# An RWKV block and a gated FFN on one core: the first block of tokens normed and mixed in two halves, sums named apart from mixes, and background work that passes what is blocked

## The chip, the core and the metric

The kernel runs on one core of a Trainium2 chip. The metric is the device time of one execution in microseconds (us). The engines are TensorE (PE in the profile; its weight loads are PEld), VectorE (DVE), ScalarE (ACT), GpSimd (POOL) and SyncE (SP). Each takes its own instructions in order. SP, ACT and POOL issue the DMAs of this kernel.

## The reference

The input has 2048 tokens of 512 channels in float32. An outer layer norm without weights stands ahead of each of two layers, and each layer is added to its input.

```
x = x + L0_attn(layernorm(x));  x = x + ffn(layernorm(x))

L0_attn(x): h = layer_norm(x, g1, b1);  hh = h shifted by one token
  k = (h*mk + hh*(1-mk)) @ Wk.T;  v, r the same with mv, mr
  x = x + sigmoid(r) * wkv(k, v) @ Wo.T
  h = layer_norm(x, g2, b2);  hh = h shifted by one token
  kk = (h*ck + hh*(1-ck)) @ Wkey.T;  kv = silu(kk) @ Wval.T
  x = x + sigmoid((h*cr + hh*(1-cr)) @ Wcr.T) * kv
ffn(h): gate, up = h @ w_gate_up.T;  (silu(gate) * up) @ w_down.T
```

So each layer begins with two norms in a row. For a token with variance v they come to (x - mean) times one inverse root of v(1+eps)+eps^2, and the residual needs the inverse root of v+eps.

## The kernel before, in words

The tokens are worked in NB = 4 blocks of 512 (NT = 4 tiles of 128 tokens). All weights are 512x512 squares, 25 of them, each kept as four quarters. A product of a block with a square is a unit. Units of the first two blocks for Wk, Wr, Wv, Wo are plain (`plain_unit`, L555): four quads (i, j) of output, where j is the half of the tokens and i the half of the output channels, and four chunks kc of 128 input channels each. One pass over a (kc, quad) pair is two calls of the matmul in L573, and the trace shows each call as two records of 128x256. A plain unit has 64 records. All other units (`unit`, L453) use seven products of half-size blocks in place of eight (56 records). For that they need sums of the activation's blocks, T1 to T4 (`sums_of`, L377: four DVE subtractions in L303), and sums of the weights, which `prepare` (L111) makes in the background and keeps in HBM. In a unit, `snapshot` (L488, ACT) copies a bank of PSUM before the next product adds to it, so PE waits for it.

The order on PE, DVE and ACT is that of the Python program (`manual_schedule`). Work that no unit needs at once is written as generators. `push` (L245) appends one to the list `background`; `urgent` (L248) puts it in front. Each unit calls `tick` (L227) after each product, or after each second chunk of a plain quad (8 ticks a plain unit). A tick adds SHARE*STEP = 0.88*1.72 = 1.51 us to an account, `slack`, capped at 2.5, takes off what was issued since, by the kernel's own cost table (0.68 for a 128x512 DVE operation), and while it is positive runs steps of `preps` or of the head of `background` (`run_one`, L165). A `yield 1` ends the tick, so that a result has time to arrive. `need` (L251) runs the head of the list, whatever the account says, until a name is in `finished`.

An entry may have a condition, `ready`. `run_one` asks it before every step of the entry, not only before the first:

```
        ready, gen, name = background[0]
        if ready is not None and not ready():
            assert not wait, name
            return False
```

For a mix it is `op_free` (L385): fewer than three of three large operand tiles are in use. A mix takes its tile in its first step (`op_tile`, L388); `op_done` gives it back when the unit that reads it issues its last product, which for a `unit` is some products later, inside the next unit (`held`, `pop_held`).

`mix` (L397) makes h*m + hh*(1-m), by chunk of channels: an ACT copy with scale (`shifted`, L406, 128x512) and a DVE multiply-add (`mixed`, in `stt`, L311). `mix_steps` (L427) then also makes the four sums, unless the unit is plain, and the name counts as finished only after them. So `need((b, name))` in `product_of` (L593) waits for the sums too.

The beginning is written out by hand. L260 loads the vectors (20 KB) on ACT's queue; L261 loads the first block of x on SP's and ACT's queues by turns; L262 to L264 load Wk, Wr, Wv. L273 issues 44 transposes of the identity (`WARM`), which nothing reads. Then `time_norm` (L624) runs for block 0 by `need("norm0")`: moments of four tiles (L317, L318), the inverse roots of 128x8 by shift, subtraction and three Newton steps on DVE (`rsqrt`, L323), four scalings (L307), 16 transposes on PE (L354), for each chunk an ACT evacuation from PSUM (L366) and, for block 0, the k mix of that chunk at once. `k_unit(0)` follows with its chunks as the outer loop. From then on norms, mixes and residuals (`residual`, L607) are background work, also those of block 1 (`norm1`).

Later, during the four up units of block b, these entries stand in the list in this order: norm b+2, mix k of b+2, residual of b+2, mix r, norm b of b+1 (`normb`), mix v of b+2, mixes cr and ck of b+1. The down unit of b follows, then the k, r and v units of b+2, then the gate unit of b+1.

Of the kernel before, what the change touches and what calls it, by code (L numbers as in the profile page):

```python
# [15 lines left out]
P = 128  # L16
H = 512
NC = H // P
# [37 lines left out]
def rwkv_ffn_kernel(  # L56
# [107 lines left out]

    def run_one(wait):  # L165

        ready, gen, name = background[0]
        if ready is not None and not ready():
            assert not wait, name
            return False  # L170
        try:
            r = next(gen)
        except StopIteration:
            background.popleft()
            finished.add(name)
            return True
        return wait or r is None
# [67 lines left out]
    def push(name, gen, ready=None):  # L245
        background.append((ready, gen, name))

    def urgent(name, gen):  # L248
        background.appendleft((None, gen, name))
# [8 lines left out]

    vec = const.tile([P, NVEC, NC], F32, name="vec")
    nc.scalar.dma_start(vec, vecs)  # L260
    xin = {0: load_x(0, (nc.sync, nc.scalar, nc.sync, nc.scalar))}  # L261
# [52 lines left out]
    def moments(src, mv):  # L314
        for t in range(NT):
            st = small.tile([P, 6], F32, tag="st", name="st")
            nc.vector.bn_stats(st, src[:, t, :])  # L317
            nc.vector.bn_aggr(mv[:, t, :], st)  # L318
            cost(512)
            cost(0)  # L320
            yield
# [39 lines left out]
    def shifted_norm(s, h, hT, g, b, then=None):  # L361
# [3 lines left out]
        def evacuate(c, pt):  # L365
            nc.scalar.activation(  # L366
                hT[:, c, 1:], pt, AF.Identity, bias=vcol(b, c), scale=vcol(g, c)
            )
            if then is not None:
                then(c)  # L370
# [17 lines left out]
    def op_tile(name):  # L388
# [3 lines left out]
        return m, [m[:, k] for k in range(7)]  # L392
# [4 lines left out]
    def mix(key, hT, row, plain=False, at_once=False):  # L397
        m, B = op_tile("mix")
        ops[key] = B

# [22 lines left out]
        if at_once:  # L423
            return lambda c: (shifted(c), mixed(c))
        return mix_steps(B, shifted, mixed, plain)

    def mix_steps(B, shifted, mixed, plain):  # L427
# [3 lines left out]
        for c in range(NC):  # L431
# [3 lines left out]
            yield  # L435
        if not plain:
            yield from sums_of(B)
# [117 lines left out]
    def plain_unit(n, B, sink, by_token, done=None, free=None, chunks_first=False):  # L555
# [4 lines left out]
        if chunks_first:  # L560
            order = [(kc, [q]) for kc in range(NC) for q in quads]
        else:
            order = [(kc, [q]) for q in quads for kc in range(NC)]
        for kc, qs in order:
            kb, k = divmod(kc, 2)
            for i, j in qs:
# [25 lines left out]

    def product_of(b, n, name, sink, by_token, done=None, free=op_done):  # L593
        if (b, name) not in ops:
            flush()
        need((b, name))
        B = ops.pop((b, name))
        if b < PLAIN and n <= WO:
            plain_unit(n, B, sink, by_token, done, free, b == 0 and name == "k")
# [7 lines left out]
    def residual(b, xb, mv, rstd):  # L607
        shift = small.tile([P, NT], F32, tag="shift", name="shift")
        tt(shift, mv[:, :, 0], rstd, ALU.mult)
        ts(shift, shift, -1.0, None, ALU.mult)  # L610
        x1 = tok_tile("x1")
        x1s[b] = x1
        for t in range(NT):
            nc.scalar.activation(
                x1[:, t, :],
                xb[:, t, :],
                AF.Identity,
                bias=shift[:, t : t + 1],
                scale=rstd[:, t : t + 1],
            )  # L620
            spent[0] += 0.4
            yield

    def time_norm(b):  # L624
# [3 lines left out]


        var = small.tile([P, 2 * NT], F32, tag="var2", name="var2")  # L630
        ts(var[:, :NT], mv[:, :, 1], EPS, None, ALU.add)
        ts(var[:, NT:], mv[:, :, 1], 1.0 + EPS, EPS * EPS, ALU.mult, ALU.add)
# [7 lines left out]
        tails[b] = residual(b, xb, mv, rstd)  # L640
        if b == 0:
            constants()
            then = mix((0, "k"), hT, MK, True, True)
            finished.add((0, "k"))
            yield from shifted_norm("a", h, hT, LN1G, LN1B, then)
        else:
            yield 1
            yield from shifted_norm("a", h, hT, LN1G, LN1B)
# [3 lines left out]
    def push_residual(b):  # L652
# [3 lines left out]
        push(("x1", b), run())  # L656
# [5 lines left out]
    def push_mix(b, name, gen):  # L662
        push((b, name), gen, op_free)
# [34 lines left out]
    def hidden_sums(key, q, plain=False):  # L698
        B = {B11: q[0, 0], B12: q[0, 1], B21: q[1, 0], B22: q[1, 1]}
        ops[key] = B  # L700
        if plain:
            finished.add(key)
        else:
            for t in (T1, T2, T4):
                B[t] = q_tile("t")
            urgent(key, sums_of(B))
# [54 lines left out]
    def up_unit(b, g):  # L761
        s = {}

        def sink(i, j, c):
# [6 lines left out]
            [ops[b, "ck"]],  # L771
# [7 lines left out]

    class Lazy:  # L780


        def __init__(self, key):
            self.key = key

        def __getitem__(self, b):
            while self.key not in ops:
                assert put_off, self.key
                flush()
            if b in (T1, T2, T3, T4):  # L790
                while self.key not in finished:
                    run_one(True)
            return ops[self.key][b]
# [23 lines left out]
    def ffn_in(b):  # L817
# [23 lines left out]
        yield from transposed(z, evacuate)  # L841
        yield 1
# [4 lines left out]
    def ffn_gate(b, g):  # L847
# [7 lines left out]
        unit([WG + g], [ops[b, "z"]], sink, False)  # L855

    def ffn_up(b, g):
        s = gated.pop((b, g))

        def sink(i, j, c):  # L860
# [4 lines left out]
            [ops[b, "z"]],  # L865
# [38 lines left out]
    push("norm0", time_norm(0))  # L904
    need("norm0")
# [21 lines left out]
    for b in range(NB):  # L927
# [28 lines left out]
        if b == NB - 1:  # L956
            push(("ffn", 0), ffn_in(0), op_free)
# [4 lines left out]
    for b in range(NB):  # L962
        for g in range(4):
            if b == 0 or g > 0:
                need(("ffn", b))
# [4 lines left out]
            if g == 1 and b + 1 < NB:  # L970
                push(("ffn", b + 1), ffn_in(b + 1), op_free)
        if b + 1 < NB:
            need(("ffn", b + 1))
# [59 lines left out]
```

## Time and profile before

| | |
|---|---|
| median of 3 runs | 1285.92 us (1285.86 to 1288.44) |
| the profiled execution | 1284.93 us, of it span 1283.2 us |
| PE busy | 1260.0 us, 98% |
| DVE, ACT, POOL busy | 51%, 27%, 9% |
| mean granted TensorE clock | 0.997 |

The span runs from the first to the last instruction; some 1.7 us of the execution lie outside it. A line of the timeline gives the start and length in us, the engine, the line of the code, the operation, the tile written and those read, how many instructions are merged, and in brackets the idle time of the engine before it with what ended that. A line of the waits gives the total in us, how often, and the longest. A line of the windows gives busy time of each engine in a stretch of the span, then the granted clock, the busy share of the DMA engines and GB/s. Records of L573 follow each other every 0.217 us on PE when nothing is missing.

### The profile page before, as it was taken

The page shows a single profiled execution, that of the slowest core. Times are in us where ns is not written, and L with a number is a line of the kernel's source. Part 1 is how long each engine was busy: PE and PEld are TensorE (multiplying, and loading weights), DVE is VectorE, ACT ScalarE, POOL GpSimd, SP SyncE. Part 2 cuts the span into 40 slices and gives each one's busy share as a digit, 9 for nine tenths or more (in the row PEclk, how much of TensorE's full clock was granted, in tenths as well). Part 3 has the DMA queues.
Part 4 walks back from the last instruction along what each step waited for, and adds up shares of the span by engine and source line. Part 5 has one row for each costly group of instructions (what it writes and reads, how often), then busy time and mean ns, then how long its engine had stood idle before and what let it go on. Part 6 is the DMA issues. An engine that isn't in the chain of part 4 may idle for free.

```text
span 1283.2 us, 16131 instructions
## 1 busy us (share of the span) xinstructions
PE 1260.0 (98%) x5900; PEld 1104.4 (86%) x5900; DVE 650.4 (51%) x1173; ACT 344.4 (27%) x579; POOL 117.7 (9%) x218
## 2 busy tenths in 40 slices
PE   8999999989999899999999999999999999999998
PEld 7788888878888788888888888888888888888886
DVE  4757667467674586733563375125631374123521
ACT  5443251343423433302311232012310122102200
POOL 1222221200121111121100000000000000000000
PEclk9999999999999999999999999999999999999999
DMA  4656787765677677688755745575456554565552
GB/s 174 237 187 201 255 265 248 240 215 172 210 237 228 225 221 236 209 281 292 235 158 178 224 148 152 155 247 152 146 151 226 176 154 145 151 178 160 155 152 70
DMA packets 121374, 251.72 MB, mean 196 GB/s; under 512 B 15056, under 2 KB 16080, under 8 KB 120272
## 3 DMA queue, kind: packets, MB, share of 16 engines
q1 hardware_dynamic: 103328, 193.51, 50.1%
q0 software_dynamic: 16960, 55.59, 11.9%
q10 hardware_dynamic: 1008, 1.59, 0.3%
q8 instruction: 48, 0.79, 0.3%
q14 instruction: 30, 0.25, 0.1%
HBM read 216.03 MB, written 34.60 MB: 195 GB/s over the span
## 4 chain that ended last, share of the span: by engine, by line
PE 95%; DVE 3%; ACT 1%; issue 0%; DMA 0%; ACTq 0%
PE ps L471 84%; PE ps L573 9%; PE ps L354 2%; DVE mix L311 1%; DVE u L303 1%; DVE mix L303 1%; DMA x<-in_x 0%; ACT s L488 0%; ACT mix L406 0%; DVE h L307 0%; DVE st L317 0%; ACT r L675 0%; DVE resid L303 0%; DVE e L303 0%; ACT e L680 0%
## 5 line engine op out<-in xcount | busy, mean ns | idle before, releaser
L471 PE MATMUL ps<-zT,w 128*128 128x256 f32 x1792 | 391.0, 379 | 0.0
L471 PEld LDWEIGHTS ps<-zT,w 128*128 128x128 f32 x1792 | 340.0, 190 | 46.0
L471 PE MATMUL ps<-mix,w 128*128 128x256 f32 x1232 | 275.4, 381 | 7.4 <-ACT s L488 5.7
L471 PEld LDWEIGHTS ps<-mix,w 128*128 128x128 f32 x1232 | 233.7, 191 | 43.2 <-ACT s L488 7.3
L471 PE MATMUL ps<-w,s 128*128 128x256 f32 x1024 | 228.0, 379 | 0.7 <-ACT u L488 0.7
L471 PEld LDWEIGHTS ps<-w,s 128*128 128x128 f32 x1024 | 194.3, 190 | 27.4 <-ACT u L488 1.1
L303 DVE TENSOR_TENSOR u<-ps,u 128x512 f32<-128x512 f32 x135 | 93.3, 691 | 227.8 <-PE ps L471 225.4
L488 ACT COPY u<-ps 128x512 f32<-128x512 f32 x136 | 79.3, 583 | 455.1 <-PE ps L471 454.9
L471 PE MATMUL ps<-w,t 128*128 128x256 f32 x816 | 181.6, 379 | 3.3 <-ACT s L488 2.5
L471 PEld LDWEIGHTS ps<-w,t 128*128 128x128 f32 x816 | 154.6, 190 | 25.2 <-ACT s L488 3.3
L303 DVE TENSOR_TENSOR s<-ps,s 128x512 f32<-128x512 f32 x84 | 57.9, 689 | 157.1 <-PE ps L471 136.1
L303 DVE TENSOR_TENSOR u<-u,u 128x512 f32<-128x512 f32 x68 | 46.8, 688 | 84.2 <-ACT u L488 84.1
L573 PE MATMUL ps<-mix,w 128*128 128x256 f32 x384 | 85.4, 385 | 4.1 <-issue 3.0
L573 PEld LDWEIGHTS ps<-mix,w 128*128 128x128 f32 x384 | 73.9, 193 | 14.8 <-issue 3.2
L128 POOL DMA_DIRECT2D sum<-raw x64 | 34.9, 546 | 262.4 <-DVE raw L303 248.4
L488 ACT COPY s<-ps 128x512 f32<-128x512 f32 x68 | 39.2, 576 | 60.4 <-PE ps L471 60.4
L881 POOL DMA_DIRECT2D out<-resid x12 | 8.6, 715 | 497.6 <-DVE resid L303 487.6
L471 PE MATMUL ps<-w,mix 128*128 128x256 f32 x224 | 51.8, 380 | 0.0
L303 DVE TENSOR_TENSOR raw<-raw 128x512 f32<-128x512 f32 x64 | 43.9, 686 | 13.4 <-DMA raw<-in_w 12.9
L471 PEld LDWEIGHTS ps<-w,mix 128*128 128x128 f32 x224 | 42.1, 190 | 6.7 <-DVE mix L311 0.7
L117 POOL DMA_DIRECT2D raw<-in_w x64 | 34.3, 542 | 124.8 <-PE ps L471 118.5
L303 DVE TENSOR_TENSOR t<-s,t 128x512 f32<-128x512 f32 x64 | 44.3, 692 | 2.1
(100 smaller groups left out, 811.2 us busy)
## 6 DMA issues: line engine op xcount, KB each, us to landing
w<-sum SPq DMA_DIRECT2D x368, 256.0 KB, 2.7
w<-in_w SPq DMA_DIRECT2D x304, 256.0 KB, 2.8
raw<-in_w POOLq DMA_DIRECT2D x64, 256.0 KB, 5.1
sum<-raw POOLq DMA_DIRECT2D x64, 256.0 KB, 3.7
q<-in_w POOLq DMA_DIRECT2D x36, 256.0 KB, 5.2
sum<-q POOLq DMA_DIRECT2D x36, 256.0 KB, 3.1
x<-in_x SPq DMA_DIRECT2D x30, 256.0 KB, 5.1
res<-x SPq DMA_DIRECT2D x4, 1024.0 KB, 6.2
```

Source lines behind the costliest of these rows:

```text
L117: paced(nc.gpsimd.dma_start(t, w[n, k]))
L128: nc.gpsimd.dma_start(sums[n][k], o)
L303: nc.vector.tensor_tensor(out, a, b, op)
L311: nc.vector.scalar_tensor_tensor(out, *args)
L354: nc.tensor.transpose(flat[:, t * P : (t + 1) * P], h[:, t, c * P : (c + 1) * P], ident)
L471: mm = nc.tensor.matmul(pz[:, m, :], lhsT=lhsT, rhs=rhs, start=first and g == 0 and m == 0 and k == 0, stop=g == last and k == 1, skip_gro ...
L488: nc.scalar.copy(tmp[name], acc["z"])
L573: mm = nc.tensor.matmul(acc[i, j][:, m, :], lhsT=act[:, k, lo] if by_token else wg[:, k, lo], rhs=wg[:, k, :] if by_token else act[:, k, : ...
L881: eng.dma_start(out_t[b][:, 2 * j : 2 * j + 2, i * HB : (i + 1) * HB], rs[b][:, 2 * j : 2 * j + 2, i * HB : (i + 1) * HB],)
```

## The change

The load of the vectors is moved behind the load of the first block of x on ACT's queue. `run_one` looks at the first three entries of the list; an entry that has begun is not asked its condition again, an entry that is not ready lets later entries with no condition, or begun ones, run, and after a `yield 1` the next entry gets a step in the same call. A mix is finished by its own name when it is mixed, and its entry, with the sums, has the name (b, name, "t"). `Lazy` (moved up, now used for all operands) runs the background until that entry is finished when a unit first asks for one of T1 to T4. Mixes and the residual get "the norm is finished" as a condition. The residual computes its shift by tile. Block 0 gets a function of its own, in place of `time_norm(0)`, and the second half of it is called by the first unit, ahead of its seventh (kc, quad) pair.

```diff
+    def step(item, wait):
+        try:
+            r = next(item[1])
+        except StopIteration:
+            background.remove(item)
+            finished.add(item[2])
+            return True
+        return True if wait or r is None else None
+
     def run_one(wait):
-        ready, gen, name = background[0]
-        if ready is not None and not ready():
-            assert not wait, name
-            return False
...
+        blocked = False
+        for item in list(background)[:3]:
+            ready = item[0]
+            if ready is not None and not item[3]:
+                if blocked or not ready():
+                    blocked = True
+                    continue
+                item[3] = True
+            if step(item, wait):
+                return True
+        assert not wait
+        return False
...
+    xin = {0: load_x(0, (nc.sync, nc.scalar, nc.sync, nc.scalar))}
     vec = const.tile([P, NVEC, NC], F32, name="vec")
     nc.scalar.dma_start(vec, vecs)
-    xin = {0: load_x(0, (nc.sync, nc.scalar, nc.sync, nc.scalar))}
...
+        finished.add(B["key"])
         if not plain:
             yield from sums_of(B)
...
-        if chunks_first:
-            order = [(kc, [q]) for kc in range(NC) for q in quads]
+        if halfway:
+            order = [(kc, [(i, j)]) for j in range(2) for kc in range(NC) for i in range(2)]
...
+            if halfway and at == 2 * NC - 2:
+                halfway()
...
+    class Lazy:
+        def __init__(self, key, plain=False):
+            self.key = key
+            self.sums = () if plain else (T1, T2, T3, T4)
+
+        def __getitem__(self, b):
+            while self.key not in ops:
+                assert put_off, self.key
+                flush()
+            if b in self.sums:
+                while (*self.key, "t") not in finished:
+                    run_one(True)
+            return ops[self.key][b]
...
-        shift = small.tile([P, NT], F32, tag="shift", name="shift")
-        tt(shift, mv[:, :, 0], rstd, ALU.mult)
-        ts(shift, shift, -1.0, None, ALU.mult)
...
+        for t, (mean, scale) in enumerate(cols):
+            shift = small.tile([P, 1], F32, tag="shift", name="shift")
+            stt(shift, mean, -1.0, scale, ALU.mult, ALU.mult)
+            nc.scalar.activation(x1[:, t, :], xb[:, t, :], AF.Identity, bias=shift, scale=scale)
...
+    def first_block():
...
+        def normed(j):
+            mv = small.tile([P, 2, 2], F32, tag="mv", name="mv")
+            yield from moments(xb[:, 2 * j : 2 * j + 2, :], mv)
+            var = small.tile([P, 4], F32, tag="var2", name="var2")
+            affine(var, mv)
+            two = small.tile([P, 4], F32, tag="two", name="two")
+            nc.gpsimd.tensor_tensor(two, var, mhalf, ALU.pow)
+            yield
+            for t in range(2):
+                cols.append((mv[:, t, 0:1], two[:, t : t + 1]))
+                ts(
+                    h[:, 2 * j + t, :],
+                    xb[:, 2 * j + t, :],
+                    mv[:, t, 0:1],
+                    two[:, 2 + t : 3 + t],
+                    ALU.subtract,
+                    ALU.mult,
+                )
+                yield
+
+        def mixed(j, other):
+            at = slice(j * HB, (j + 1) * HB)
+            by_one = slice(j * HB + 1, (j + 1) * HB + 1)
+            for c in range(NC):
+                pt = bank()
+                for t in range(2):
+                    nc.tensor.transpose(
+                        pt[:, 0, t * P : (t + 1) * P],
+                        h[:, 2 * j + t, c * P : (c + 1) * P],
+                        ident,
+                    )
+                nc.scalar.activation(
+                    hT[:, c, by_one],
+                    pt[:, 0, :],
+                    AF.Identity,
+                    bias=vcol(LN1B, c),
+                    scale=vcol(LN1G, c),
+                )
+                d = m[:, 2 * (c // 2) + j, c % 2, :]
+                nc.scalar.activation(d, hT[:, c, at], AF.Copy, scale=onem[:, 0, c : c + 1])
+                stt(d, hT[:, c, by_one], vcol(MK, c), d, ALU.mult, ALU.add)
+                next(other, None)
+
+        one, two = normed(0), normed(1)
+        for _ in range(3):
+            next(one)
+        next(two)
+        for _ in one:
+            pass
+        constants()
+        nc.vector.tensor_copy(hT[:, :, 0:1], carry["a"])
+        next(two)
+        next(two)
+        mixed(0, two)
+        for _ in two:
+            pass
+
+        def second():
+            mixed(1, iter(()))
+            tails[0] = residual(0, xb, cols)
+            nc.vector.tensor_copy(carry["a"], hT[:, :, TB : TB + 1])
+            finished.add("norm0")
+            slack[0] = spent[0] = 0.0
+
+        return second
...
     def push_mix(b, name, gen):
-        push((b, name), gen, op_free)
+        norm = f"normb{b}" if name in ("cr", "ck") else f"norm{b}"
+        push((b, name, "t"), gen, lambda: norm in finished and op_free())
...
-    push("norm0", time_norm(0))
-    need("norm0")
+    second_half = first_block()
```

`affine` holds the two operations of L631 and L632, on two tiles at a time in block 0. In the same way as for the mixes, `ffn_gate` and `ffn_up` read their operand through `Lazy`, and the FFN waits with `need((b, "z"))` for the transposed operand without its sums.

## Prediction

> **What bounds the kernel.** I read the page's busy times first: PE is busy for 1260.0 of 1283.2 us, and the forty slices show nothing but 8 and 9 for it. So only PE's idle time, about 23 us, and time in which its clock is low can be won. The waits of PE say what ended the idle time:
>
> ```profile
> PE ps L471 <- ACT s L488: 8.2, 5, 3.0
> PE ps L573 <- issue: 3.0, 1, 3.0
> ```
>
> The timeline of PE alone, over the whole span, puts places to them (start, length, and in brackets the idle time before):
>
> ```profile
> 15.11 41.71 PE L573 MATMUL ps<-mix,w 128*128 128x256 f32 x192 [1.11 <-DVE mix L311]
> ...
> 61.57 15.74 PE L573 MATMUL ps<-mix,w 128*128 128x256 f32 x64 [3.01 <-issue]
> ...
> 270.62 3.90 PE L471 MATMUL ps<-mix,w 128*128 128x256 f32 x16 [0.83 <-PE ps L471]
> ...
> 277.55 8.58 PE L471 MATMUL ps<-mix,w 128*128 128x256 f32 x32 [3.03 <-ACT s L488]
> ...
> 304.90 1.96 PE L471 MATMUL ps<-w,t 128*128 128x256 f32 x8 [1.28 <-ACT s L488]
> ...
> 445.77 7.17 PE L471 MATMUL ps<-mix,w 128*128 128x256 f32 x32 [2.43 <-ACT s L488]
> ```
>
> See three kinds: 15.11 us before the first product; 3.01 us ahead of block 1's k unit; and a triple (270.62, 277.55, 304.90) in and after block 2's r and v units. Block 3 has the triple again: 0.83 at 439.44, the 2.43 shown, 1.25 at 472.01. Windows around the two longest waits add a cost (granted clock after the busy times):
>
> ```profile
> 61.50:63.00 1.50, 1.43 (x4) 1.18 (x5) 1.50 (x3) 1.50 (x3) 0.00 (x0) 0.66 0.00 0
> 63.00:65.00 2.00, 2.00 (x6) 1.64 (x5) 2.00 (x4) 0.74 (x2) 0.54 (x1) 0.50 0.00 0
> 65.00:67.00 2.00, 2.00 (x9) 1.71 (x9) 0.38 (x1) 0.01 (x1) 0.00 (x0) 0.90 0.34 131
> ...
> 277.50:279.00 1.50, 1.45 (x4) 1.18 (x5) 1.47 (x4) 1.50 (x4) 0.00 (x0) 0.50 0.00 0
> 279.00:281.00 2.00, 2.00 (x7) 1.66 (x6) 0.68 (x2) 0.22 (x2) 0.00 (x0) 0.64 0.00 0
> ```
>
> After a wait of 3.0 us the clock is down: 1.5*0.34 + 2*0.50 + 2*0.10 = 1.7 us lost at 61.5, and 1.5*0.50 + 2*0.36 = 1.5 at 277.5. After the 2.43 us, in 446 to 448, it stays at 1.00.
>
> Why those waits? ACT's timeline of the beginning shows a mix that stops halfway:
>
> ```profile
> 17.81 4.40 ACT L406 ACTIVATE mix<-hT_a,onem 128x512 f32<-128x512 f32 x7
> ...
> 34.85 1.32 ACT L406 ACTIVATE mix<-hT_a,onem 128x512 f32<-128x512 f32 x2
> ```
>
> The seven are k's last chunk, r's four and v's first two; v's other two come 12.6 us later. v took the third operand tile in its first step, then `ready` was asked again and saw three in use: the entry blocks itself, and all behind it, until k gives its tile back. By the bookkeeping five of k's eight ticks run nothing. The same happens to r and v of blocks 2 and 3. So v's mix is done under `need`, and its sums with it; DVE there:
>
> ```profile
> 269.76 1.41 DVE L311 SCALAR_TENSOR_TENSOR mix<-hT_a,vec,mix 128x512 f32<-128x512 f32 x2 [1.59 <-ACT mix L406]
> 271.10 0.69 DVE L303 TENSOR_TENSOR raw<-raw 128x512 f32<-128x512 f32 x1
> 271.70 2.74 DVE L303 TENSOR_TENSOR mix<-mix 128x512 f32<-128x512 f32 x4
> ```
>
> Four sums stand ahead of the subtraction that ACT, and then the snapshot for PE, wait for.
>
> **Part A, the beginning.** Removed: the 2.2 us of `rsqrt` (11 small instructions, 8.17 to 10.39). DVE in the new order: tile 0 has arrived at 3.72 as before; tile 1's load is issued 0.44 earlier (1.18 to 0.74, where the vectors stood), so I put its moments at 4.9 instead of 5.36 and their end at 5.75; `affine` 0.25; tile 2's moments 0.80 to 6.9; two scalings 1.0 to 7.9; constants and carry 0.4; tile 3's moments and `affine` 1.1 to 9.4. The vectors' load is now third on ACT's queue, issued near 1.66; with the 3.1 to 5.0 us that this queue's loads took it lands by 6.7, before `constants`. Nothing of Wr's moves, since as many issues stand ahead of it.
>
> The two powers on POOL are in no row. Nearest rows: memset 128x1 0.09, affine select 128x128 0.29; upper end 1.6, the select with an engine's load of tables (1.28 on ACT) in front; below nothing they cannot be, being added work. I take 0.3. The first lies under tile 2's 0.8 us of moments, and up to 2.1 us would be free for another reason: PE is in its 44 warm-up transposes until 9.30, whatever DVE does. The second has from 9.4 to 11.2. POOL's next work, DMA issues, came at 29.5.
>
> So PE decides: two transposes at 9.30 (the warm-up's line is 1.36 and 7.94 long), ACT 0.48 later (12.36 to 12.73 for one, plus 0.11), an evacuation of half size, 0.79 less 256 columns at the 0.27 us that separates 128x512 from 128x256 = 0.52, a copy 0.45, the multiply-add 0.48, handovers 0.1: first product at 11.3 instead of 15.11. Then a chunk costs ACT 0.9 and PE 8*0.217 = 1.74, so PE does not wait. The second half's eight transposes (8*0.109 = 0.87, under the first products' wait before) now lie inside the products, at 16.5; their first mix is ready near 18.5, while PE has the seventh and eighth pair until 19.1. k ends at 26.1 instead of 29.0: **-2.9**. Ends: -3.5 and 0 (both powers at their upper end together with a late tile 1).
>
> The Trainium skill speaks against this part: the GPSIMD Engine Reference, section Instruction dispatch, says that the first call of a freshly loaded kernel pays about 6 us for loading its code, and its Engine selection gives elementwise work to VectorE. No row here shows such a load. By that figure I estimate the first product at about 15 and part A at +1.
>
> r's mix now starts after the second half. ACT has 8 halves to 20.7, a sink of 2.05, four copies 2.5, a residual 0.74, two copies 1.3, to 27.3; the last chunk is mixed by 28.1, and PE needs it at 26.1+3*0.87 = 28.7. I count 0, with 1.5 as the other end.
>
> **Part B, block 1's k unit.** By the bookkeeping the mix of v and the residual now run in k's ticks, some 5 us of account earlier, so norm 1 and k's mix are issued before the v unit ends, where before the last transposes and the mix stood under `need`. 3.0 + 1.7 = 4.7 us go. What is late next is DVE. From 27.3 ACT has three sinks, two copies and a residual, 8.2 us, to 35.5, and DVE's last k operation waits for them until 36.1. Behind it stand three moments (2.4), `affine` and `rsqrt` (2.5), four scalings (1.9), five sums of weights, four operations of r's sinks and one of v's at 0.6 in the ticks' order (6.0), less 0.6 of pipelining: 12.2, to 48.3, while PE reaches the transposes in v's fourth tick, 26.1 + 13.9 + 4*1.74 = 46.9: 1.4 back, I take 1.5. **-3.2**, ends -4.7 and 0.
>
> **Parts C and D, blocks 2 and 3.** v's mix runs during the down unit. But cr's mix then takes v's place when k's tile comes free, ck's takes cr's: the bursts of four mixes stay, the four sums (2.74) no longer stand in them, since `need` asks for the mix alone and the sums spread over ticks. I leave the 0.83 waits and half a microsecond each time. Block 2: 3.03 + 1.47 + 1.28 - 0.5 = **-5.3** (ends -6.6, 0). Block 3: 2.43 + 1.25 - 0.4 = **-3.3** (ends -4.5, 0).
>
> At nothing: the residual's shift, four DVE operations of 0.17 instead of two, 0.35 a block, hidden by DVE's idle half (0.35 where DVE is late). The FFN's and channel norm's names: no wait of PE lies between 474 and 1263 us. A `yield 1` no longer ends a tick when the next entry can run; where k's mix begins with the residual behind it, or r's with `normb`, DVE can come to a multiply-add whose copy ACT has not made. Waits of 1.59 on that are in the fence above. I count 0, other end in the rivals.
>
> **Sum.** -2.9 - 3.2 - 5.3 - 3.3 = -14.7 against the profiled execution's 1284.93 (span 1283.2 and 1.7 outside): 1270.2. The median is 1.0 above that execution, so 1271.2.
>
> **Rivals.**
> 1. *The start gives nothing*: powers or handovers hold DVE until the gain of A is gone, and r's mix comes late. For it: no row of a power, a thin ACT margin at 28. Against: 2 us of cover by the warm-up. 1274.1, up to 1275.6 with the 1.5 of r.
> 2. *The waits only move up a unit*: cr's and ck's bursts meet the same snapshots, C and D are lost. For it: the 0.83 waits come from copies, not sums. Against: the 2.74 us of sums ahead of 277.55. 1271.2 + 8.6 = 1279.8.
> 3. *Slower*: in the up units of blocks 0 and 1, where mixes of k and r begin with another entry behind them, a multiply-add blocks DVE behind an ACT copy that itself stands behind a sink waiting for DVE's earlier work; PE waits 3 us and the clock falls, 3.0 + 1.7 = 4.7 a place. Four places make 18.8, 1290.0; it decides from 14.7 us on, which is a little over three such places. Against: PE has no wait there now, and the copies are issued one entry earlier than the multiply-add.
> 4. *Nothing happens*: the list is seldom blocked and gains in one unit are waited for in the next, 1285.9. Against: PE is the bound, and few of its waits hang on DMA.
>
> **Numbers.** Forecast 0.57, rival 1 0.18, rival 2 0.15, rival 3 0.07, rival 4 0.03. Best ends together: -3.5 - 4.7 - 6.6 - 4.5 = -19.3, 1266.6; I reach to 1265, as tile 1 may come earlier still. Upwards rival 2 is taken in: 1281. About 0.2%, 2.6 us, is what a measurement of this kernel can tell from no change. Faster 0.57+0.18+0.15 = 0.90, same 0.03, slower 0.07.
>
> **What would show it.** First record of L573 near 11.3, transposes at 9.3; POOL's power under 1 us; no idle time and no clock under 0.9 at block 1's k unit, or up to 1.5 us at its transposes; v's last copies on ACT before the k unit's second half ends; in the v units of blocks 2 and 3 multiply-adds of hT_b where hT_a stood, and no wait above 1 us. A power of several us, a wait of 3 us with the clock at half, or new waits in the up units would make the prediction wrong.

## The result, and the profile after

The changed kernel takes **1278.95 us** in the median of six runs (1275.75 to 1280.47), the kernel before 1285.89 beside it (six runs, 1282.71 to 1288.44): ratio 0.9943, interval 0.9926 to 0.9961. It is faster by 6.9 us, where the forecast had 14.7. The profiled execution takes 1277.33 us, span 1275.5, mean granted clock 0.997; PE is busy for 1257.2 us instead of 1260.0.

To see which part gave what, I cut both spans at the moments at which SP issues the store of a block's residual (`res<-x`, after the down unit of blocks 0, 1, 2). The windows between these moments give PE's busy time, and the rest is idle:

| stretch | before: length, busy, idle | changed: length, busy, idle | difference | forecast |
|---|---|---|---|---|
| start to block 0's store | 256.28, 248.46, 7.82 | 249.35, 245.44, 3.91 | -6.93 | A + B: -6.1 |
| to block 1's store (r, v and out units of block 2 lie here) | 168.52, 163.38, 5.14 | 165.95, 162.78, 3.17 | -2.57 | C: -5.3 |
| to block 2's store (the same units of block 3) | 165.37, 160.83, 4.54 | 167.15, 161.60, 5.55 | **+1.78** | D: -3.3 |
| to the end | 693.03, 687.37, 5.66 | 693.05, 687.36, 5.69 | +0.02 | 0 |

The beginning is as forecast (a little better); C gave half, and D went the wrong way. The profiled execution is one of the faster ones of its kernel, 1.6 us under its median; why runs differ by such steps is said at the end. PE's timeline of the changed kernel, over the whole span (as before: start, length, and in brackets the idle time ahead):

```profile
1.37 7.29 PE L286 MATMUL warm<-ident 128*128 128x128 f32 x44 [1.37 <-POOL ident masks.py:199]
10.85 5.45 PE L583 MATMUL ps<-mix,w 128*128 128x256 f32 x24 [1.06 <-DVE mix L323]
47.51 0.33 PE L366 MATMUL ps<-ident,h 128*128 128x128 f32 x1 [0.72 <-DVE h L319]
48.56 1.64 PE L366 MATMUL ps<-ident,h 128*128 128x128 f32 x13 [0.72 <-DVE h L319]
268.41 8.86 PE L478 MATMUL ps<-mix,w 128*128 128x256 f32 x32 [2.31 <-ACT s L495]
295.39 1.96 PE L478 MATMUL ps<-w,t 128*128 128x256 f32 x8 [0.85 <-ACT sr L857]
435.31 8.86 PE L478 MATMUL ps<-mix,w 128*128 128x256 f32 x32 [2.97 <-ACT s L495]
463.82 1.97 PE L478 MATMUL ps<-w,t 128*128 128x256 f32 x8 [2.38 <-issue]
```

Read it against the list of before. The 3.01 at block 1's k unit is gone, and two waits of 0.72 stand at its transposes (47.51, 48.56). Both waits of 0.83 are gone. But of the two long waits each has a follower, 2.31 (3.03 before) and 2.97 (2.43 before), and 32 records that take 7.17 at full clock take 8.86 after both. The out units' waits are 0.85 (1.28) and 2.38 (1.25). The windows show the clock behind the first of them:

```profile
268.40:270.00 1.60, 1.59 (x5) 1.30 (x6) 1.57 (x4) 0.46 (x1) 0.00 (x0) 0.65 0.00 0
270.00:272.00 2.00, 2.00 (x7) 1.55 (x6) 1.97 (x4) 0.19 (x1) 0.00 (x0) 0.50 0.00 0
272.00:274.00 2.00, 2.00 (x10) 1.79 (x9) 1.22 (x2) 0.40 (x1) 0.00 (x0) 0.93 0.49 130
```

1.6*0.35 + 2*0.50 + 2*0.07 = 1.7 us are lost there, and 8.86 - 7.17 = 1.7 the second time; before, block 3's 2.43 had cost no clock.

What stands in DVE's order ahead of the 2.97 wait (PE is idle from 432.34 to 435.31), in DVE's timeline:

```profile
425.47 0.69 DVE L315 TENSOR_TENSOR u<-ps,u 128x512 f32<-128x512 f32 x1 [1.37 <-PE ps L478]
429.07 1.41 DVE L323 SCALAR_TENSOR_TENSOR mix<-hT_b,vec,mix 128x512 f32<-128x512 f32 x2 [2.91 <-ACT mix L417]
430.78 1.42 DVE L323 SCALAR_TENSOR_TENSOR mix<-hT_b,vec,mix 128x512 f32<-128x512 f32 x2 [0.29 <-ACT mix L417]
432.11 0.69 DVE L323 SCALAR_TENSOR_TENSOR e<-e,r 128x512 f32<-128x512 f32 x1
432.71 0.68 DVE L315 TENSOR_TENSOR u<-u,u 128x512 f32<-128x512 f32 x1
```

The mix is of hT_b: it is cr's mix of block 2, four multiply-adds in one piece, ahead of the subtraction `u<-u,u`. The next product hangs on that subtraction by way of ACT, whose work in that order is the activation of the subtraction's result and then the snapshot (it ends at 435.26, and PE starts at 435.31):

```profile
434.16 0.63 ACT L796 ACTIVATE sg<-u 128x512 f32<-128x512 f32 x1 [2.80 <-DVE u L315]
434.69 0.57 ACT L495 COPY s<-ps 128x512 f32<-128x512 f32 x1
```

Ahead of the 2.31 wait (PE is idle from 266.10 to 268.41) stand three multiply-adds of cr's mix of block 1; the fourth comes only at 269.86:

```profile
262.84 1.41 DVE L323 SCALAR_TENSOR_TENSOR mix<-hT_b,vec,mix 128x512 f32<-128x512 f32 x2 [2.32 <-ACT mix L417]
264.54 0.75 DVE L323 SCALAR_TENSOR_TENSOR mix<-hT_b,vec,mix 128x512 f32<-128x512 f32 x1 [0.29 <-ACT mix L417]
...
265.81 0.68 DVE L315 TENSOR_TENSOR u<-u,u 128x512 f32<-128x512 f32 x1
```

By the bookkeeping the entry of cr's mix starts when k's operand tile comes free in the r unit, with the account at its cap.

The beginning in DVE's timeline (the first two lines are the moments of tiles 0 and 1, the last is the two scalings that wait for the power):

```profile
4.61 0.69 DVE L329 BATCH_NORM_STATS2 st<-x 128x6 f32<-128x512 f32 x1 [3.65 <-DMA x<-in_x]
...
5.44 0.66 DVE L329 BATCH_NORM_STATS2 st<-x 128x6 f32<-128x512 f32 x1
...
7.75 1.00 DVE L319 TENSOR_SCALAR h<-x,mv,two 128x512 f32<-128x512 f32 x2 [0.35 <-POOL two L692]
```

and POOL's timeline, with the operation of which before had no row:

```profile
6.67 1.04 POOL L692 TENSOR_TENSOR two<-var,mhalf 128x4 f32<-128x4 f32 x1 [5.36 <-DVE var L319]
```

### The profile page after: what moved, and what is told of

The parts are those of the page before. It is cut to its first block, busy times and chain, and to the rows that moved or that the text cites. A ratio compares the mean times of both kernels' runs of the same rounds, so it can differ in the third digit from the quotient of the medians.

```text
span 1275.5 us, 16147 instructions
## 1 busy us (share of the span) xinstructions
PE 1257.2 (99%) x5900; PEld 1104.8 (87%) x5900; DVE 649.6 (51%) x1177; ACT 347.1 (27%) x587; POOL 121.5 (10%) x220
## 4 chain that ended last, share of the span: by engine, by line
PE 94%; ACT 3%; DVE 2%; issue 1%; POOL 0%; POOLq 0%
PE ps L478 86%; PE ps L583 6%; PE ps L366 1%; ACT mix L417 1%; PE warm L286 1%; DVE u L315 0%; DVE mix L323 0%; ACT r L778 0%; ACT e L783 0%; DVE e L323 0%; ACT x L644 0%; ACT mix L725 0%; ACT hT_a L717 0%; DVE q L315 0%; DVE h L319 0%
```

## The experiments

Two theories. **Theory 1**: cr's mix takes the place of v's in a burst (several operations issued in one piece), and the sums apart from the mix do what the forecast said of them (they keep 2.74 us out of the bursts). **Theory 2**, the rival: the names do harm, since sums that are asked for at their first use come late. The first four kernels take the change apart, the others price single steps and put together what helped. "Marks" are the three stores above.

| kernel | median us (range, runs) | ratio to before (interval) | marks of the profiled run |
|---|---|---|---|
| first block only | 1282.17 (1278.54 to 1285.05, 7) | 0.9965 (0.9948 to 0.9982) | 253.22, 422.00, 587.36 |
| list and names only | 1277.67 (1276.63 to 1281.2, 4) | 0.9941 (0.992 to 0.9962) | 251.06, 414.96, 582.09 |
| sums asked for at need | 1273.55 (1272.11 to 1273.67, 4) | 0.9901 (0.9886 to 0.9917) | 249.25, 414.04, 578.59 |
| paced mixes | 1269.82 (1269.7 to 1271.4, 4) | 0.9874 (0.9857 to 0.9892) | 251.05, 413.25, 576.53 |
| only g at need | 1273.63 (1272.98 to 1273.65, 4) | 0.9900 (0.9884 to 0.9917) | 251.03, 415.88, 578.74 |
| roots on DVE | 1281.8 (1281.1 to 1283.88, 6) | 0.9968 (0.9957 to 0.998) | 254.72, 420.30, 589.03 |
| first chunk paced, g at need | 1270.61 (1268.74 to 1272.18, 4) | 0.9878 (0.9863 to 0.9893) | 249.38, 410.85, 575.60 |
| all paced, g at need | 1270.1 (1268.27 to 1271.52, 4) | 0.9874 (0.9859 to 0.9888) | 250.97, 412.43, 576.67 |
| the same, start filled | 1269.84 (1269.67 to 1270.17, 4) | 0.9877 (0.9859 to 0.9896) | 249.63, 411.09, 575.32 |
| all paced, g and cr at need | **1266.56** (1266.15 to 1267.92, 4) | 0.9855 (0.9832 to 0.9878) | 249.26, 410.72, 571.25 |
| vectors first | 1276.98 (one run) | | 249.00, 414.95, 582.10 |

The kernel before had medians of 1285.96, 1286.08 and 1285.66 beside the three sets.

**First block only.** The list is as before; the beginning is the changed one.

```diff
-        for item in list(background)[:3]:
+        for item in list(background)[:1]:
             ready = item[0]
...
+            if ready is not None and not ready():
+                assert not wait, item[2]
+                return False
+            return step(item, wait) or False
...
+            need((b, name, "t"))
...
```

> The changed beginning alone: block 0 in halves with the power on GpSimd and the vectors' load behind x; the list is again asked at its head only and before every step, and a unit's need waits for the mix and its sums. Marks are the issues of the stores of blocks 0, 1 and 2 after their down units (before 256.28, 424.80, 590.17 us; changed kernel 249.35, 415.30, 582.45). Theory (the beginning is worth 3.3 by itself, the list the rest): first product at 10.9, a wait of about 3 us with half clock ahead of block 1's k unit again, marks 253.0, 421.5, 586.9, total 1282.6. Rival (the beginning only moves what block 1's norm waits for): the first product is at 10.9 too, but the wait ahead of block 1's k unit grows by as much, first mark at 256, total 1286.

Measured: the first store 3.06 earlier than in the kernel before, the two stretches behind it 168.78 and 165.36, as before (168.52, 165.37). So part A alone is worth 3.1, and nothing of it is lost or won later.

**List and names only.** The beginning of before (vectors first, four tiles, roots on DVE, chunks outer), the rest as changed.

```diff
+    vec = const.tile([P, NVEC, NC], F32, name="vec")
+    nc.scalar.dma_start(vec, vecs)
     xin = {0: load_x(0, (nc.sync, nc.scalar, nc.sync, nc.scalar))}
...
+        for _ in rsqrt(var, two, 2 * NT):
+            pass
...
```

> The list, the names and the residual as changed, with the beginning of the kernel before (all four tiles normed together, inverse roots on VectorE, chunks as the outer loop of the first unit, vectors loaded first). Theory (the parts add): first product at 15.1, no wait or one under 1.5 us at block 1's norm, first mark at 252.7, then the changed kernel's own gain of 2.6 and loss of 1.8: marks 418.6 and 585.8, total 1281. Rival (the list's gain at block 1 needs the early start): a wait of 3 us and half clock ahead of block 1's k unit as before, first mark at 256.

Measured: -5.22 at the first store. Both parts alone make -8.28, together -6.93: the 1.35 between them are about the two waits of 0.72 at block 1's transposes, which neither of these two kernels has. On top of the list, then, the new beginning is worth 251.06 - 249.35 = 1.7 at the first store, and the medians do not show even that: the list alone takes 1277.67, both together 1278.95, and their ranges overlap. The rest of this kernel has the waits of the changed one (2.31, 0.50, 2.96, 2.38), but behind its 2.31 the clock stays up:

```profile
270.11 7.17 PE L478 MATMUL ps<-mix,w 128*128 128x256 f32 x32 [2.31 <-ACT s L495]
```

**Sums asked for at need.** The names stay, but every unit asks for mix and sums together, as before the change.

```diff
-        if name != "g":
-            need((b, name))
+        if (b, name) == (0, "k"):
+            need((b, name))
+        elif name != "g" or not plain:
+            need((b, name, "t"))
...
```

> The changed kernel with one part undone: a unit's need waits for the whole entry, mix and sums, as before the change. Theory (the sums' names are worth little, since the list already lets v's mix end during the down unit; what waits in blocks 2 and 3 is the burst of cr's mix): waits of 2.3 and 3.0 us in the v units stay, marks within 1 us of 249.35, 415.30, 582.45, total 1279 to 1280. Rival (sums that are asked for only at their first use put VectorE late, which makes the 2.38 us wait in block 3's out unit): that wait shrinks below 1.3, the last mark comes 1.5 earlier, total 1277.

Measured: 1273.55, 5.4 us under the changed kernel, where I had expected it no faster. Theory 1 falls in its second half. The waits 2.31 and 2.97 stay to a hundredth (so no sum of v or cr had been kept out of them by the names), and the waits of the out units, 0.85 and 2.38, are gone.

**Only g at need.** The out unit reads g, which the v unit leaves. In the changed kernel no `need` is made for it, and the first use of one of its sums runs the list.

```diff
+        elif not plain:
+            need((b, name, "t"))
```

> The changed kernel, but the out unit's need runs the four sums of its operand (g) before its first product; the mixes' sums stay apart as changed. Before this the whole of the names was undone and the time fell to 1273.55, which spoke for the late sums as a cost. Theory (all of that is g: its sums are put into the list where VectorE meets operations that wait for PE first, and PE then waits for the sums): no wait in the out units of blocks 2 and 3 (0.85 and 2.38 in the changed kernel), marks 249.3, 414.0, 578.6, total 1273.5. Rival (cr's sums have a share): the second wait stays above 1, total 1275 to 1277.

Measured: 1273.63, within the ranges the same as with all names undone (1273.55), so it is g alone. DVE's timeline of the changed kernel around the wait of 2.38, and of this kernel at the same place (`t<-e` and `t<-e,t` are g's sums):

```profile
460.98 0.69 DVE L315 TENSOR_TENSOR s<-ps,s 128x512 f32<-128x512 f32 x1 [1.17 <-ACT s L495]
461.70 0.69 DVE L315 TENSOR_TENSOR x<-s,x 128x512 f32<-128x512 f32 x1
462.31 0.68 DVE L315 TENSOR_TENSOR t<-e 128x512 f32<-128x512 f32 x1
463.03 1.42 DVE L315 TENSOR_TENSOR t<-e,t 128x512 f32<-128x512 f32 x2
```

```profile
458.62 0.68 DVE L315 TENSOR_TENSOR t<-e 128x512 f32<-128x512 f32 x1
459.33 1.42 DVE L315 TENSOR_TENSOR t<-e,t 128x512 f32<-128x512 f32 x2
...
461.87 0.69 DVE L315 TENSOR_TENSOR s<-ps,s 128x512 f32<-128x512 f32 x1
```

In the changed kernel the sums stand behind `s<-ps,s`, which waits for PE's product and ACT's copy of it; asked for at the head of the unit they stand in front. The two waits make 3.23 of the 5.3 us. The rest can be the clock: in the kernel with the roots on DVE, whose wait at this place is 2.39, eight records take 3.55 after it and not 1.97. That the changed kernel's other runs lose this 1.6 too is likely from their clocks (0.996 in the median runs, 0.997 in the profiled one), but no trace of them shows it.

**Paced mixes.** As changed, but cr's and ck's mixes of blocks 1 and 2 issue one copy and one multiply-add a tick.

```diff
...
+        if key[1] in ("cr", "ck") and key[0] in (1, 2):
+            shifted(0)
+            yield 1
+            for c in range(NC):
+                mixed(c)
+                if c + 1 < NC:
+                    shifted(c + 1)
+                yield 1
+        else:
...
```

> The changed kernel, but in the cr and ck mixes of blocks 1 and 2 one copy stands a step ahead of its multiply-add and every step ends its turn, so that a tick issues one chunk and not three or four. Theory (PE's waits in the v units come from the burst: multiply-adds that wait on VectorE for copies, ahead of the subtraction that ScalarE's snapshot hangs on): the waits of 2.3 and 3.0 us go below 0.5 with no clock under 0.9 behind them, marks 249.4, 411.5, 573.5, total about 1270. Rival (VectorE simply has too much to do there, whatever the order): the waits move on to the gate and out units, marks within 2 us of the changed kernel's, total 1277 to 1279.

Measured: 1269.82, 9.1 us under the changed kernel. PE's timeline:

```profile
268.40 7.17 PE L487 MATMUL ps<-mix,w 128*128 128x256 f32 x32 [0.60 <-ACT s L504]
...
430.90 7.17 PE L487 MATMUL ps<-mix,w 128*128 128x256 f32 x32 [0.60 <-ACT s L504]
...
445.54 3.69 PE L487 MATMUL ps<-w,mix 128*128 128x256 f32 x16 [2.29 <-issue]
```

and DVE's, to be held against the lines of the changed kernel above:

```profile
427.03 0.75 DVE L323 SCALAR_TENSOR_TENSOR mix<-hT_b,vec,mix 128x512 f32<-128x512 f32 x1 [2.91 <-ACT mix L417]
427.69 0.69 DVE L323 SCALAR_TENSOR_TENSOR e<-e,r 128x512 f32<-128x512 f32 x1
428.30 0.69 DVE L315 TENSOR_TENSOR u<-u,u 128x512 f32<-128x512 f32 x1
```

The 2.91 that DVE waits for the first copy are the same in both. From the first multiply-add to the subtraction it is 432.71 - 429.07 = 3.64 in the changed kernel and 428.30 - 427.03 = 1.27 here: 2.37 less, and PE's wait is 2.97 - 0.60 = 2.37 shorter. So three multiply-adds and the 0.29 between them are the whole difference, and DVE's wait for ACT is no part of it. In block 2 it is the same: 2.97 from the first of three to the subtraction, 1.28 with one (264.53 to 265.81), and PE waits 2.31 - 0.60 = 1.71 less. With the waits went the half clock, and of the out units' waits 0.50 each is left. A new wait of 2.29 stands in block 2's gate unit (445.54, above); here it costs no clock, and its cause comes out below. The 9.1 is a difference of medians. In the two profiles the stretches behind the first store are 7.6 shorter (3.75 and 3.87), and the stretch ahead of it is 1.7 longer, since the clock of this run fell at the beginning (24 records in 7.13).

**Roots on DVE.** The power on POOL is replaced by the eleven small instructions of `rsqrt`, in halves.

```diff
...
-            nc.gpsimd.tensor_tensor(two, var, mhalf, ALU.pow)
+            for _ in rsqrt(var, two, 4):
+                pass
```

> The changed kernel with the two powers of the first block on VectorE again, by shift and Newton steps on 128x4, in the place where the power was issued. Theory (the power took 1.04 and is nearly covered; the eleven small operations take 2.2 each time and stand ahead of the first multiply-add): first product at 14.9 instead of 10.85, first mark 249.35 + 4.0 less the 1.4 us wait at block 1's transposes that the early start causes = 252.0, total 1281. Rival (halves alone give the start): first product before 12.5, total within 1 us of the changed kernel.

Measured: the first product at 14.45, 3.6 later than the changed kernel's, so the two powers are worth 3.6 there. The first store comes 5.37 later, since the clock is at 0.50 from 12 to 18 and 24 records take 7.22 instead of 5.45: PE had been idle for 2.24 us ahead of the transposes and for 2.75 behind them.

```profile
14.45 7.22 PE L583 MATMUL ps<-mix,w 128*128 128x256 f32 x24 [2.75 <-DVE mix L323]
```

**First chunk paced, g at need.** Only cr's first chunk is paced; the others follow in one piece.

```diff
+        one = key[1] == "cr" and key[0] in (1, 2)
...
+            if one and c == 0:
+                shifted(1)
+                shifted(2)
+                yield 1
+                continue
...
```

> The changed kernel with g's sums at need, and cr's mixes of blocks 1 and 2 issuing one chunk in the tick where the tile comes free, the rest as changed. Theory (only the multiply-adds that stand ahead of one subtraction on VectorE cost): waits in the v units 0.6, none in the out units; block 3's gate unit may wait up to 2.3 for cr's last sums; marks 249.3, 411.0, 574, total 1268. Rival (a burst that is broken up once comes back in the next unit): the v unit's wait goes to 0.6, but waits of 1 to 2 us appear in both gate units, total above 1271.

**All paced, g at need.** The edits of the paced kernel and of "only g at need" together.

> Paced cr and ck mixes of blocks 1 and 2, one chunk a tick, and g's sums at need. Theory (the two remedies add: 4.6 us of the paced mixes without g's 0.5 us waits): waits 0.6 in the v units, 2.3 in block 3's gate unit, none in the out units; total 1269. Rival (with ck's chunks spread into the out unit, the sums of g at need come late there): waits of 1 us or more in the out units, total 1270 to 1272.

Measured: 1270.61 and 1270.1, which the ranges do not tell from the 1269.82 of pacing alone. From the changed kernel pacing took 9.1 and g 5.3, both together 8.9, not 14.4. The two overlap (pacing had left 0.50 of each of g's waits), and the two kernels have waits of 2.03 and 2.29 in block 2's gate unit, with the clock down after them (in the expectations it is called block 3's, since it follows block 3's v unit). PE's timeline of the second:

```profile
444.74 5.38 PE L487 MATMUL ps<-w,mix 128*128 128x256 f32 x16 [2.29 <-issue]
```

and DVE's there, cr's sums being `mix<-mix`:

```profile
443.35 0.68 DVE L315 TENSOR_TENSOR raw<-raw 128x512 f32<-128x512 f32 x1
443.95 2.01 DVE L315 TENSOR_TENSOR mix<-mix 128x512 f32<-128x512 f32 x3
```

Between the first sum, at 439.50, and the other three stand five operations on PE's products and one sum of the weights: g's mistake once more, and it is in the paced kernel too.

**All paced, g and cr at need.** On top of "all paced":

```diff
-        if name != "g":
+        if name == "cr":
+            need((b, name, "t"))
+        elif name != "g":
             need((b, name))
```

> As the all-paced kernel, but cr's sums are asked for with cr's mix at the head of the gate unit. Theory: the 2.29 us that PE waits at 444.74, inside the gate unit after block 1's store, come from cr's last sums being asked for at the first use of one of them, behind other DVE work; asked for one product earlier (1.74 us) they are done in time: wait 0.6 at most there, the clock not below 0.9 after it, 2.3 - 0.6 + 1.7 = 3.4 us less between the second and third store, median 1266.7. Rival: they were issued as early as DVE allowed, and the wait only moves to the unit's first product: a wait of 1.5 to 2.3 us one or two products earlier, median 1270.1.

Measured: 1266.56, as the theory had it. The wait and the low clock are gone (1.00 from 440 to 450); DVE has the sums together at the head of the unit:

```profile
437.78 2.74 DVE L315 TENSOR_TENSOR mix<-mix 128x512 f32<-128x512 f32 x4
440.44 0.68 DVE L315 TENSOR_TENSOR u<-u,u 128x512 f32<-128x512 f32 x1
```

This is the fastest kernel here: 19.1 us under the kernel before, 12.4 under the changed one.

**The same as "all paced", start filled.** Eight transposes of the identity that nothing reads, behind the first half's eight.

```diff
+            if j == 0:
+                pt = bank()
+                for _ in range(8):
+                    nc.tensor.transpose(pt[:, 0, 0:P], ident, ident)
```

> As the all-paced kernel, with eight more transposes of the identity on PE after the first half's eight, in a bank that nothing reads. Theory: PE's idle 1.06 us between 9.7 and 10.8, with the thin work before it, is what let the clock fall to half there (24 records in 7.13 us instead of 5.45). The eight take 8*0.109 = 0.87 us, end near 10.6, and delay nothing: first product 10.8 to 10.9, clock 1.00 from 10 to 18, 24 records in 5.45, the first block's store at 249.3 instead of 250.97, median 1270.1 - 1.6 = 1268.5, and no run in the upper step. Rival, the fall belongs to the run and not to that gap: the dip stays in some runs, median 1270.1. Rival, the extra transposes come late (behind a bank that is not free): first product above 11.2, median 1270.5.

Measured: inconclusive. PE's idle time ahead of the first product falls from 1.06 to 0.19, and the clock is 1.00 from 8 to 18. But the kernel with cr at need has the 1.06 and no low clock in its profile either (24 records in 5.45), and the median did not move (1269.84 against 1270.1). Nor was this run's warm-up short (7.81 us), as it was in the three profiles with 24 records in 7.13 (6.36 to 6.52).

**Vectors first.** The changed kernel with the two loads in their old order.

```diff
-    xin = {0: load_x(0, (nc.sync, nc.scalar, nc.sync, nc.scalar))}
     vec = const.tile([P, NVEC, NC], F32, name="vec")
     nc.scalar.dma_start(vec, vecs)
+    xin = {0: load_x(0, (nc.sync, nc.scalar, nc.sync, nc.scalar))}
```

> The changed kernel with the load of the vectors in front of the load of x again, as before. Theory: x had nothing from its place in front, since all loads that start together share what the queues move: tile 0's first moments at 3.7 instead of 4.61, the first product within 0.2 of 10.85, time within 1 us of 1277.3, plus or minus the 1.6 of a clock step. Rival, the move is worth what I gave it (tile 1 some 0.4 us earlier): the first product at 11.2 or later and the moments of tile 1 0.4 us later than 5.5 to 6.3.

Measured, in one run: tile 0's moments at 3.56, tile 1's at 5.04, the first product at 10.49, 0.36 before the changed kernel's and more than the 0.2 that the theory allowed. The eight profiles with x in front, the power on POOL and no extra transposes have the first product at 10.74 to 11.02. So the move of x to the front is no gain, and by this run a small loss; why the loads land as they do is not shown.

```profile
3.56 0.69 DVE L329 BATCH_NORM_STATS2 st<-x 128x6 f32<-128x512 f32 x1 [2.59 <-DMA x<-in_x]
...
5.04 0.69 DVE L329 BATCH_NORM_STATS2 st<-x 128x6 f32<-128x512 f32 x1 [0.57 <-DMA x<-in_x]
```

## Why the prediction was right and wrong

**Part A** was right in its sum, -2.9 against the -3.06 of the first block alone, though three of its terms were off; that they cancelled is luck. Tile 1 did not come earlier: with x in front tile 0 came at 4.61 instead of 3.72, and the second moments ended at 6.31 instead of 5.75. The power took 1.04 and not 0.3; DVE waited 0.35 and 0.39 for it. Against that the warm-up ended at 8.66 and not at 9.30 (its length varies from 6.36 to 7.94 in the kernels here), so PE was no bound until 9.30: the first `h` was done near 8.3, and the first product came at 10.85, under the 11.3 forecast. The estimate from the GPSIMD Engine Reference of the Trainium skill, section Instruction dispatch, a first product near 15, is not what this run shows: the first power took 1.04, the second 1.01.

**Part B** was right: 3.01 and 1.7 gone, 1.44 back at the transposes, where PE waits for DVE's scalings, as worked out (1.5).

**Parts C and D** failed, and the step is this one: "the bursts of four mixes stay, the four sums (2.74) no longer stand in them, since `need` asks for the mix alone and the sums spread over ticks. I leave the 0.83 waits and half a microsecond each time." It holds two errors.

First, half a microsecond was far too little for a burst without sums. The prediction had seen that cr's mix takes v's place, and rival 2 had said what comes of it; but the wait was credited to the four sums alone, as if multiply-adds in the same place cost nothing. Three of them are 2.97 us from the first to the subtraction in block 2, four are 3.64 in block 3, and PE waited 2.31 and 2.97, each with 1.7 us of half clock in the profile. Pacing, which changes only how cr's and ck's mixes are issued, takes both waits to 0.60, by just the multiply-adds that left the piece, so the chain from burst to wait is shown, not only argued. The 0.83 that I left went instead.

Second, the names were booked as the gain, and they are a loss of about 5.3 us in the medians. v's sums were out of the way without them, since the list lets its mix run in the down unit: the kernel that asks for everything at need has the very same 2.31 and 2.97. What the names did alter was the out unit's operand g, which the prediction did not look at: its sums moved behind operations that wait for PE, 0.85 and 2.38.

With the measured prices the step gives for block 2 idle time 2.31 + 0.85 instead of 5.14 and a clock loss of 1.7 instead of 1.5, -1.8 (measured -2.57); for block 3 idle time 2.97 + 2.38 instead of 4.51 and 1.7 where there was none, +2.5 (measured +1.78). In both stretches the measured change is 0.8 us lower than that. Most of it is in PE's rows of the kernel before, at a granted clock of 1.00: in block 2, 72 records from 253.88 take 15.92, 16 from 270.62 take 3.90 and 16 from 285.97 take 3.83, some 0.7 more than at the pace of the changed kernel's rows (88 records in 19.16, 16 in 3.62). What held them there is open.

**Rival 2** (1279.8), to which the prediction gave 0.15, is nearest to what came: its mechanism, cr's burst before the same snapshots, is the one that pacing confirms. That its number fits 1278.95 so well is in part luck. It had C and D at nothing, and they came to -2.57 and +1.78; and without g's late sums, which no rival had, the kernel takes 1273.6, nearer to the forecast. Rivals 1, 3 and 4 did not come: the start gave its gain, and no wait of PE stands in the up units of blocks 0 and 1.

## What to carry to other kernels

When work in a queue is let past what blocks it, ask what it will do when the block goes: here it started with a full account and put three or four operations into one engine's order at once, ahead of what was due next. Price that burst by all its operations, not by the part that the change removes, and try what it gives to let such an entry issue one operation a tick (9.1 us here). And a wait that is moved from the head of a unit to the first use of a result can be a loss on an engine that works in order: here the work then stood behind operations that wait for the very unit that needs it, and that took 5.3 us.

## What the runs showed of the hardware

The granted clock after a wait is no function of the wait's length alone. After 2.31 us it fell to 0.50 in the changed kernel and stayed at 1.00 in the kernel with the list alone; after 2.97 it fell in the changed kernel and not in "only g at need":

```profile
435.89 7.17 PE L478 MATMUL ps<-mix,w 128*128 128x256 f32 x32 [2.97 <-ACT s L495]
```

What decides is where the wait lies. In windows of 0.1 us each fall behind a unit's wait lasts 3.41 us (so it costs some 1.7), and in the nine profiles with two falls or more the falls lie whole multiples of 3.413 us apart: at 268.89 and 436.14 in the changed kernel (49 times), at 11.24, 274.07, 441.32 and 468.63 with the roots on DVE (77, 126 and 134 times). So each of these runs has a fixed grid of 3.413 us, and the clock falls at a line of it. Behind the waits of the units, in all these kernels, it fell 18 times, and each time PE had been idle for 2.00 to 3.03 us of the 3.41 ahead of the fall. Where less of a piece of the grid was idle the clock stayed at 1.00: 1.89 in the kernel with the list alone, whose 2.31 is cut in two by a line, 1.67 in "only g at need", whose 2.97 is, and 1.49 in the kernel before, at block 3's 2.43. (One piece with 2.01 idle, at the changed kernel's wait of 2.38, stayed at 1.00 too, so the bound lies close to 2.0.) No unit's wait under 2.0 us was followed by a fall. Where the grid lies against the waits differs from run to run, so the same wait costs clock in one run and not in the next, and runs of one kernel lie in steps: the changed kernel's at 1275.75, 1277.33, four from 1278.91 to 1280.47, with mean clocks of 0.998, 0.997, and 0.996 to 0.994.

A page of the Trainium skill, TensorE: Matmul & The Clock Gate, section What's actually happening, says that the activity window, some 3.4 us, runs free of the program; the grid agrees with that. Its section HAM oscillation asks for no idle gaps over about 3.4 us; here gaps of 2.03 to 3.03 were enough, so the measurement sets the bound lower. A single profile of a kernel with waits of 2 to 3 us is 1.7 us uncertain for each of them.

At the beginning, where PE does transposes between its waits, an idle 1.06 ahead of the first product was followed by half clock in three profiles (24 records in 7.13) and by full clock in six (5.45). The three are those with the shortest warm-up lines (6.36 to 6.52 us against 6.69 to 7.60), in which PE also waited 0.41 to 0.63 ahead of its first transposes; of the six only "first block only" has such a wait (0.45).

A power of 128x4 on POOL takes 1.04 us the first time and 1.01 the second. Eleven dependent operations of 0.16 us on DVE come every 0.2 us and take 2.2 in all (6.65 to 8.8 with the roots on DVE), so the one slow operation is shorter than the chain, and DVE is free for other work meanwhile. And tile 0's moments began at 4.47 to 4.81 where both queues began with x, at 3.56 to 3.77 where one began with the vectors, while tile 1's began at 5.30 to 5.64 and at 5.04 to 5.36.
